# Decoder of twelve sublayers on one core: the last part of the middle sublayers (rank-gated layer, factored attention) stepped between the heads of the second cross attention

## The chip, the cores and the metric

The kernel runs on one core of one Trainium2 chip, in one launch. The metric is the device time in microseconds (us) from launch to end. The core has a matrix engine (TensorE, PE in the profile, with its weight loads as PEld), a vector engine (VectorE, DVE), a scalar engine (ScalarE, ACT), a general engine (GpSimd, POOL) and a queue engine that issues transfers (SyncE, SP). Each engine works through its own list of instructions in the order in which the built program has them. Matrix products land in PSUM, in banks; everything else lives in SBUF.

## The reference

A pre-norm decoder over `x` of shape (8, 256, 128), with a context of shape (8, 512, 128). Every sublayer is `x = x + f(layernorm(x))`:

```
x = x + L0_attn (linear attention)        x = x + L0_xattn (16 heads, context, mask)
x = x + L0_ffn  (8 experts, top 2)
x = x + L1_attn (causal over the 8 batches, rotary)
x = x + L1_xattn (one head, context)
x = x + L1_ffn:  xr, xk = mixes of x and the token before it
                 out = sigmoid(xr Wr) * (relu(xk Wk)^2 Wv)
x = x + L2_attn: qkv = x Wqkv + b; each token sees at most 9 tokens (offsets 0, 1, 2, 4 .. 128)
                 softmax over those, 16 heads of 8, then a projection
x = x + L2_xattn (16 heads of 8, context of 512 keys, no mask)
x = x + L2_ffn  (quantised)
x = x + L3_attn, L3_xattn (16 causal heads each), L3_ffn (3 low-rank blocks)
```

L1_ffn is the rank-gated layer of the title and L2_attn the factored attention. Neither mixes batches: L1_ffn looks one token back in its own batch, L2_attn at most 128 tokens back in its own batch. So batch b of L2_xattn needs only batch b of all that comes before it.

## The kernel before, in words

The running `x` stays in SBUF, and `xt(b)` holds its normalised transpose for batch b. A sublayer ends for a batch with `_norm` (statistics on DVE, the root on POOL, the scaling on DVE) and `_normed` (transposes on PE into `ln_ps`, a copy to `xt` on ACT). The tiles of a sublayer have a two-letter prefix: `moe_` L0_ffn, `ra_` L1_attn, `xa_` L1_xattn, `rk_` L1_ffn, `fa_` L2_attn, `mh_` the head attentions, `qf_` L2_ffn. L0_ffn to L2_attn are called the middle sublayers. Each works in four groups of two batches, and `_middle` runs them as a diagonal: at step s sublayer k does group s - k, the later sublayers first. So L2_attn's four groups come at s = 4 to 7, and at s = 7 only its last group is left. Written as calls, from the end of L0_ffn on: fa(0), rk(1), xa(2), ra(3); fa(1), rk(2), xa(3); fa(2), rk(3); then `E.draining()`, which opens L2_xattn; then fa(3).

A group of L2_attn has four units of 128 tokens. A unit's `weigh` makes q (`fa_qps`, `fa_q`), then up to 9 shifted keys and values, two offsets to a bank (`fa_kvps`): DVE multiplies keys by q (`fa_pr`), ACT copies values (`fa_v`). Then come DVE reductions and a softmax (`fa_sc`, `fa_red`, with an exponential on ACT), and POOL multiplies the values by the weights (`fa_v`). `apply` sums them on DVE (`fa_o`), turns the result (`fa_tps`, `fa_ot`), projects it (`fa_yps`) and adds it to `x`. In the middle the PSUM banks are: three for L0_ffn and then for L2_attn, four for the other sublayers, one for the norms.

L2_xattn is `_heads_attention`. Its loop runs over t = 16 b + h, one head of one batch to a step, 128 steps and 12 more to drain. At step t it computes head t's scores on PE (`mh_sps`) and takes their maxima on DVE (`mh_nm`, two per step); 8 steps later it computes the scores again with the maxima in them (`mh_bsps`) and takes the exponentials on ACT (`mh_e`); 4 steps later, once in four steps, it multiplies by the values (`mh_ops`). Keys, queries and values of batch b+1 are made while batch b runs (`steps`: `mh_kps`, `mh_qps`, `mh_vps`, and transfers on SP that spread them over heads). All of this program's matmuls go through `hd.mm`, which keeps them in program order, and all its other banks come from one pool of two, `hd_g`:

```
self.g = ctx.enter_context(E.tc.tile_pool(name="hd_g", bufs=2, space=PSUM, side="right"))
```

Before its first head, `begin` fills the tiles for keys, queries and values with constants on ACT (`fills`, eight copies from `plain`, four before the first batch's keys and four after), and makes batch 0's keys, values and queries.

The loop can take a guest: a generator of which it runs a few steps between two heads. L0_xattn has one, the rest of L0_attn:

```
normed_already = set(range(B)) if guest is None else {0}
...
        if guest:
            visit(2.4 if t < 9 else 1.4)
```

`visit(r)` adds r to a credit and takes one step of the guest for every whole one. The guest yields a batch's number when that batch's `xt` is ready; before the loop makes batch b+1's queries it runs the guest until that number has come. Order within an engine is otherwise set by the framework's scheduler, from the program order and the dependences.

Of the kernel before, what the change touches and what calls it, by code (L numbers as in the profile page):

```python
# [40 lines left out]
P = 128  # L41
# [176 lines left out]
def _layer_norm(E, b, psum):  # L218
    _normed(E, b, _norm(E, b), psum)


# [235 lines left out]

def _heads_attention(E, ctx, causal=False, mask=None, key_bias=None, gate=False, guest=None):

# [193 lines left out]

    normed_already = set(range(B)) if guest is None else {0}
    credit = [0.0]
# [11 lines left out]
    while t < end or todo:  # L667
        now[0] = t
        b, h = divmod(t, H)
        if b + 1 < B:  # L670
            if h == 0:
                early, spread, values = hd.steps(b + 1)
            if causal:

                at = {2: early[:1], 3: early[1:2], 4: early[2:], 13: [values]}
                at.update({5 + i: spread[i : i + 1] for i in range(6)})
            else:
                at = {6: early[:1], 8: spread[:1], 9: spread[1:2] + early[1:], 13: spread[5:] + [values]}
                at.update({10 + i: spread[2 + i : 3 + i] for i in range(3)})
            if not causal and h == 9:  # L680
                while b + 1 not in normed_already:
                    visit(1)
            for f in at.get(h, ()):
                f()
        if gate and b < B and h == 6:
            gate_of(b)
        if t < H * B:
            maxima(t)
            if t % 4 == 3:
                turn(t // 4)  # L690
        if guest:
            visit(2.4 if t < 9 else 1.4)
        if t % 4 == 1 and 4 < t < H * B + 2:
            turned(t // 4 - 1)
        if 0 <= t - lag < H * B:
            exps(t - lag)
        c = t - lag - 4
        if c % 4 == 0 and 0 <= c < H * B:
            combine(c // 4)
        for f in todo.pop(t, ()):  # L700
            f()
        if t == H * (B - 2) + 12 + free:
            E.draining()
        t += 1
# [50 lines left out]
def _l2_xattn(E, ctx):  # L755
    _heads_attention(E, ctx)

# [255 lines left out]

def _l1_ffn(E, ctx, pg):
    nc, W = E.nc, E.w("L1_ffn")
    one = ctx.enter_context(E.tc.tile_pool(name="rk1", bufs=1, side="right"))
    wk = ctx.enter_context(E.tc.tile_pool(name="rk", bufs=2, side="right"))
    rest = one.tile([P, 2], F32, name="rk_rest")
    for i, n in enumerate(("mu_r", "mu_k")):
        nc.vector.tensor_scalar(rest[:, i : i + 1], W(n), -1.0, 1.0, ALU.mult, ALU.add)  # L1020
    mixed = {}

    def mix(g):
        for i, n in enumerate(("mu_r", "mu_k")):
# [3 lines left out]
            nc.vector.scalar_tensor_tensor(m, E.xt2(g), W(n), t, ALU.mult, ALU.add)  # L1028
            mixed[g, i] = m.rearrange("p b t -> p (b t)")

    def channels(g):
        mr, mk = mixed.pop((g, 0)), mixed.pop((g, 1))
        ps = pg.tile([P, 512], F32, tag="g", name="rk_kps")
        nc.tensor.matmul(ps, W("wk"), mk, start=True, stop=True)
        k = wk.tile([P, 512], F32, name="rk_k")
        nc.scalar.activation(k, ps, AF.Relu)
        nc.scalar.activation(k, k, AF.Square)
        ps = pg.tile([P, 4, D], F32, tag="g", name="rk_rps")
        for t in range(4):
            nc.tensor.matmul(ps[:, t, :], mr[:, t * P : t * P + P], W("wr"), start=True, stop=True)  # L1040
        r = wk.tile([P, 4, D], F32, name="rk_r")
        nc.scalar.activation(r, ps, AF.Sigmoid)
        ps = pg.tile([P, 4, D], F32, tag="g", name="rk_ops")
        for t in range(4):
            nc.tensor.matmul(ps[:, t, :], k[:, t * P : t * P + P], W("wv"), start=True, stop=True)
        nc.vector.tensor_tensor(r, ps, r, ALU.mult)
        for b in range(2):
            E.add(2 * g + b, r[:, 2 * b : 2 * b + 2, :])
            _layer_norm(E, 2 * g + b, E.mid_ln)

    def unit(g):
        mix(g)
        channels(g)

    return unit


def _l2_attn(E, ctx, pg):

# [8 lines left out]
    def weigh(t):  # L1068
# [5 lines left out]
        no = len(offs)  # L1074
        ps = pg.tile([P, D], F32, tag="g", name="fa_qps")
        nc.tensor.matmul(ps, E.xt(b)[:, at], W("wqkv")[:, :D], start=True, stop=True)
        q = wk.tile([P, D], F32, name="fa_q")
        nc.vector.tensor_tensor(q, ps, W("b")[:, :D], ALU.add)

        qb = wk.tile([P, D], F32, tag="fa_s", name="fa_qb")  # L1080
        nc.gpsimd.tensor_tensor(qb, q, W("b")[:, D : 2 * D], ALU.mult)
        pr = wk.tile([P, NO, D], F32, name="fa_pr")
        v = wk.tile([P, NO, D], F32, name="fa_v")
        for i in range(0, no, 2):
            n = min(2, no - i)
            ps = pg.tile([P, 2, 2 * D], F32, tag="g", name="fa_kvps")
            for j in range(n):
                nc.tensor.matmul(ps[:, j, :], E.xt(b, offs[i + j])[:, at], W("wqkv")[:, D:], start=True, stop=True)  # L1088
            nc.vector.tensor_tensor(
                pr[:, i : i + n, :], ps[:, :n, :D], q.unsqueeze(1).to_broadcast([P, n, D]), ALU.mult  # L1090
            )
            nc.scalar.copy(v[:, i : i + n, :], ps[:, :n, D:])  # L1092
        sb = wk.tile([P, H], F32, name="fa_sb")
        nc.vector.tensor_reduce(sb, heads(qb), AX.X, ALU.add)
# [18 lines left out]
    def apply(t):  # L1113
# [3 lines left out]
        nc.vector.tensor_tensor(o, o, W("b")[:, 2 * D :], ALU.add)  # L1117
        ps = pg.tile([P, P], F32, tag="g", name="fa_tps")
        nc.tensor.transpose(ps, o, E.ident)
        ot = wk.tile([P, P], F32, name="fa_ot")  # L1120
        nc.scalar.copy(ot, ps)
        ps = pg.tile([P, D], F32, tag="g", name="fa_yps")
        nc.tensor.matmul(ps, ot, W("wo"), start=True, stop=True)
        nc.vector.tensor_tensor(E.x[:, t, :], ps, E.x[:, t, :], ALU.add)
        if t % 2:
            _layer_norm(E, t // 2, E.mid_ln)

    return lambda g: _pipeline(4, lambda i: weigh(4 * g + i), lambda i: apply(4 * g + i))


def _middle(E, names):


    with ExitStack() as last, ExitStack() as scope, ExitStack() as early:
        banks = lambda to, name, bufs, side="left": to.enter_context(
            E.tc.tile_pool(name=name, bufs=bufs, space=PSUM, side=side)
        )
        E.mid_ln = banks(last, "mid_ln", 1)
        mid = banks(scope, "mid_pg", 4, "right")
        moe = banks(early, "moe_pg", 3) if "L0_ffn" in names else None  # L1140
        units = {}
        for n in names:
            if n != "L2_attn":
                units[n] = MIDDLE[n](E, scope, moe if n == "L0_ffn" else mid)
        for s in range(len(names) + 3):
            for k in reversed(range(len(names))):
                if not 0 <= s - k < 4:
                    continue
                if names[k] == "L2_attn":
                    if s == k:  # L1150
                        early.close()
                        units["L2_attn"] = _l2_attn(E, last, banks(last, "fa_pg", 3))
                    if s == k + 3:
                        scope.close()
                        E.draining()
                units[names[k]](s - k)

# [123 lines left out]
def _l3_ffn(E, ctx):  # L1281
# [90 lines left out]
}  # L1372
MIDDLE = {
    "L0_ffn": _l0_ffn, "L1_attn": _l1_attn, "L1_xattn": _l1_xattn, "L1_ffn": _l1_ffn, "L2_attn": _l2_attn,
}


@with_exitstack
def kernel(ctx: ExitStack, tc: tile.TileContext, ins, at, out, layers=ALL):
# [128 lines left out]

    def prefetch(layer):

        if not small:
            small.append(ctx.enter_context(tc.tile_pool(name="small", bufs=2)))
        if layer in ("L0_ffn", "L3_ffn"):
            load(layer, big.enter_context(tc.tile_pool(name="big", bufs=1)))
        elif layer:
            load(layer, small[0], tag="w")

    if kind(layers[0]) != "L0":
        prefetch(layers[0])
    for i, part in enumerate(parts):  # L1520
        layer, following = part[0], parts[i + 1][0] if i + 1 < len(parts) else None
        E.draining = lambda: begin(following)
        if kind(layer) == "L0":

            def given_up():
                first_w.close()
                prefetch(following)

# [4 lines left out]
        if kind(layer) == "middle":  # L1533
            hd.close()
            E.heads = None
            with tc.tile_pool(name="mid_w", bufs=1) as pool:
                for n in part[1:]:
                    load(n, pool)
                prefetch(following)
                _middle(E, part)  # L1540
            big.close()
            continue
        prefetch(following)
        begin(layer)
# [28 lines left out]
```

## Time and profile before

| | |
|---|---|
| median of 3 runs | 1841.8 us (1839.02 to 1846.99) |
| the profiled execution | 1841.85 us, of which the span from first to last instruction is 1840.1 us |
| busy: PE, DVE, ACT, POOL | 1492.4, 1175.7, 876.6, 489.3 us |
| mean granted TensorE clock | 0.902 |
| first `mh_sps` of L2_xattn | at 1043.8 us |

Times in the trace are us from the start of the span. Rows give the busy time of an engine in a stretch, the mean of one instruction in ns, and the idle time of an engine before a group of instructions with what ended it. Ends of matmuls are modelled, so the distance between two starts is the better measure of what one costs.

### The profile page before, as it was taken

The page shows a single profiled execution, that of the slowest core. Times are in us where ns is not written, and L with a number is a line of the kernel's source. Part 1 is how long each engine was busy: PE and PEld are TensorE (multiplying, and loading weights), DVE is VectorE, ACT ScalarE, POOL GpSimd, SP SyncE. Part 2 cuts the span into 40 slices and gives each one's busy share as a digit, 9 for nine tenths or more (in the row PEclk, how much of TensorE's full clock was granted, in tenths as well). Part 3 has the DMA queues.
Part 4 walks back from the last instruction along what each step waited for, and adds up shares of the span by engine and source line. Part 5 has one row for each costly group of instructions (what it writes and reads, how often), then busy time and mean ns, then how long its engine had stood idle before and what let it go on. Part 6 is the DMA issues. An engine that isn't in the chain of part 4 may idle for free. (4 is left out here: it accounts for less than half of the span.)

```text
span 1840.1 us, 29268 instructions
## 1 busy us (share of the span) xinstructions
PE 1492.4 (81%) x10099; PEld 1071.3 (58%) x10137; DVE 1175.7 (64%) x3843; ACT 876.6 (48%) x1789; POOL 489.3 (27%) x986
## 2 busy tenths in 40 slices
PE   5689999999989988884664689999634999899976
PEld 3466677776655655552453366666413777677753
DVE  4567666666557576788785766666584665455546
ACT  7245445555633434331336266766321666466621
POOL 3222212212101022124233221221225333344321
PEclk9899999999999999886786799999865999899977
DMA  4011101114000000000001021211001321111000
GB/s 149 12 35 34 25 14 36 35 35 156 5 1 1 1 1 1 1 1 0 1 1 34 11 61 37 68 39 37 17 24 54 88 56 48 46 51 49 26 1 23
DMA packets 47235, 60.42 MB, mean 33 GB/s; under 512 B 5232, under 2 KB 36976, under 8 KB 46448
## 3 DMA queue, kind: packets, MB, share of 16 engines
q1 hardware_dynamic: 44720, 56.99, 11.6%
q8 instruction: 80, 1.31, 0.3%
q10 hardware_dynamic: 2368, 1.57, 0.3%
q14 instruction: 67, 0.55, 0.1%
HBM read 14.50 MB, written 1.05 MB: 8 GB/s over the span
## 5 line engine op out<-in xcount | busy, mean ns | idle before, releaser
L443 PE MATMUL mh_sps<-mh_k,mh_q 96*128 96x512 f32 (+2 forms) x1024 | 323.0, 398 | 36.0 <-DMA mh_q<-mh_qp 17.5
L443 PE MATMUL mh_bsps<-mh_q,mh_k 128*128 128x256 f32 (+1 forms) x1536 | 341.3, 327 | 2.8 <-DMA mh_q<-mh_m 1.5
L575 ACT ACTIVATE mh_e<-mh_bsps 128x512 f32<-128x512 f32 x512 | 276.2, 598 | 96.1 <-PE mh_bsps L443 86.5
L443 PEld LDWEIGHTS mh_bsps<-mh_q,mh_k 128*128 128x128 f32 x1536 | 263.6, 194 | 29.7 <-issue 6.5
L443 PEld LDWEIGHTS mh_sps<-mh_k,mh_q 96*128 96x128 f32 x1024 | 172.4, 201 | 89.1 <-issue 34.6
L502 DVE CUSTOM_DVE_ANT_0 mh_rest<-mh_sps,mask_b 128x512 bf16<-128x512 f32 x256 | 167.2, 684 | 82.1 <-PE mh_sps L443 78.9
L443 PE MATMUL mh_ops<-mh_e,mh_v 128*32 128x256 f32 (+1 forms) x3072 | 204.8, 377 | 10.7 <-ACT mh_e L562 10.6
L521 DVE TENSOR_REDUCE mh_nm<-mh_sps 128x1 f32<-128x512 f32 x256 | 159.9, 682 | 59.7 <-PE mh_sps L443 59.7
L443 PEld LDWEIGHTS mh_ops<-mh_e,mh_v 128*32 128x32 f32 x3072 | 97.5, 112 | 82.8 <-ACT mh_e L562 22.0
L562 ACT ACTIVATE mh_e<-mh_bsps 128x384 f32<-128x384 f32 x256 | 116.5, 494 | 49.5 <-PE mh_bsps L443 29.8
L197 POOL TENSOR_SCALAR ln_rstd<-ln_mv 128x2 f32<-128x2 f32 x96 | 22.5, 237 | 412.7 <-DVE ln_mv L195 402.0
L502 DVE CUSTOM_DVE_ANT_0 mh_rest<-mh_sps,km_q 128x128 bf16<-128x128 f32 (+1 forms) x256 | 80.0, 350 | 66.3 <-PE mh_sps L443 64.5
L502 DVE CUSTOM_DVE_ANT_0 mh_rest<-mh_sps,causal 128x128 bf16<-128x128 f32 (+1 forms) x256 | 79.5, 353 | 63.1 <-PE mh_sps L443 46.0
L528 POOL CAST mh_hi<-mh_nm 128x8 fp32r<-128x8 f32 x128 | 24.6, 192 | 333.6 <-DVE mh_nm L502 203.8
L215 ACT COPY xt<-ln_ps 128x256 f32<-128x256 f32 x96 | 36.2, 377 | 151.1 <-PE ln_ps L214 99.0
L214 PE MATMUL ln_ps<-ident,ln_z 128*128 128x128 f32 x100 | 30.3, 370 | 84.4 <-DVE ln_z L201 82.1
L605 ACT COPY mh_osb<-mh_ops 128x256 f32<-128x256 f32 x128 | 47.7, 373 | 102.4 <-PE mh_ops L443 102.3
L1088 PE MATMUL fa_kvps<-w_L_attn,xt 128*128 128x256 f32 x272 | 83.6, 457 | 13.6 <-ACT fa_v L1092 10.3
L540 ACT CAST mh_m<-mh_mps 8x256 fp32r<-8x256 f32 x128 | 46.3, 362 | 98.4 <-PE mh_mps L446 95.8
L443 PE MATMUL mh_bsps<-mask_t,ident 128*128 128x512 bf16 x219 | 85.2, 389 | 0.4 <-ACT mh_e L575 0.4
L863 ACT ACTIVATE moe_si<-moe_gps 128x512 f32<-128x512 f32 x64 | 38.0, 597 | 97.8 <-PE moe_gps L861 74.1
L214 PEld LDWEIGHTS ln_ps<-ident,ln_z 128*128 128x128 f32 x100 | 15.2, 162 | 107.1 <-DVE ln_z L201 62.3
(339 smaller groups left out, 3166.3 us busy)
## 6 DMA issues: line engine op xcount, KB each, us to landing
mh_k<-mh_kp SPq DMA_DIRECT2D x64, 256.0 KB
mh_q<-mh_qp SPq DMA_DIRECT2D x256, 64.0 KB
mh_k<-mh_kp SPq DMA_DIRECT2D x64, 128.0 KB
w_L_ffn<-in_w_L_ffn SPq DMA_DIRECT2D x2, 1558.0 KB
w_L_attn<-in_w_L_attn SPq DMA_DIRECT2D x2, 1056.0 KB
ctx_t<-in_ctx_t SPq DMA_DIRECT2D x4, 512.0 KB
mh_q<-mh_m ACTq DMA_DIRECT2D x128, 8.0 KB
w_L_ffn<-in_w_L_ffn SPq DMA_DIRECT2D x2, 687.0 KB
```

What stands on the lines that cost most here:

```text
L214: E.nc.tensor.transpose(ps[:, q, :], z[:, q, :], E.ident)
L215: E.nc.scalar.copy(E.xt(b), ps.rearrange("p q t -> p (q t)"))
L443: return self.E.tc.keep_in_program_order(self.E.nc.tensor.matmul(*a, **kw))
L502: nc.vector.tensor_tensor_reduce(rest[:, : scores.shape[1]], scores, lowered, -1.0, -FLOOR, ALU.add, ALU.min, accum_out=at)
L521: nc.vector.tensor_reduce(u.nm[:, c, col], ps, AX.X, ALU.max, negate=True)
L528: nc.gpsimd.tensor_copy(hi, nm)
L540: nc.scalar.copy(m, ps[:8].rearrange("p c q -> p (c q)"))
L562: nc.scalar.activation(e, ps, AF.Exp, scale=scale)
L575: nc.scalar.activation(e, ps, AF.Exp, scale=scale)
L605: nc.scalar.copy(osbs[b][:, u4 % 2, :], ops)
L863: nc.scalar.activation(si, pgate, AF.Silu)
L1088: nc.tensor.matmul(ps[:, j, :], E.xt(b, offs[i + j])[:, at], W("wqkv")[:, D:], start=True, stop=True)
```

## The change

`_l1_ffn` and `_l2_attn` become generators that yield between pieces: L2_attn after the queries, after each bank of keys and values and around the projection; L1_ffn after the mix, after each product and around the norms. `_middle` writes its order out: the diagonal as it was up to fa(0), then rk(1), xa(2), ra(3), xa(3). The rest, fa(1), rk(2), fa(2), rk(3), fa(3), is left in one generator, `E.guest`, and L2_xattn runs it between its heads, with batches 0 and 1 known as ready. In that part the tiles come from `hd_g` and the matmuls go through `hd.mm`. L1_ffn's work tiles have one buffer in place of two. L2_xattn is opened when `_middle` has returned, no longer before fa(3). The weights of all middle sublayers are loaded in L0's last part, ahead of L0_ffn's own, where they came after them.

```diff
-def _heads_attention(E, ctx, causal=False, mask=None, key_bias=None, gate=False, guest=None):
+def _heads_attention(E, ctx, causal=False, mask=None, key_bias=None, gate=False, guest=None, known=(0,)):
...
-    normed_already = set(range(B)) if guest is None else {0}
+    normed_already = set(range(B) if guest is None else known)
...
-            visit(2.4 if t < 9 else 1.4)
+            visit(2.4 if t < 9 and 1 not in known else 1.4)
...
 def _l2_xattn(E, ctx):
-    _heads_attention(E, ctx)
+    guest, E.guest = E.guest, None
+    _heads_attention(E, ctx, guest=guest, known=(0, 1))
...
-def _l1_ffn(E, ctx, pg):
+def _l1_ffn(E, ctx, side="left"):
-    wk = ctx.enter_context(E.tc.tile_pool(name="rk", bufs=2, side="right"))
+    wk = ctx.enter_context(E.tc.tile_pool(name="rk", bufs=1, side=side))
...
+        yield
+        mr, mk = mixed
+        ps = E.banks.rk.tile([P, 512], F32, tag="g", name="rk_kps")
+        E.mm(ps, W("wk"), mk, start=True, stop=True)
...
         for b in range(2):
             E.add(2 * g + b, r[:, 2 * b : 2 * b + 2, :])
-            _layer_norm(E, 2 * g + b, E.mid_ln)
+            zs.append(_norm(E, 2 * g + b))
+        yield
+        yield
+        for b in range(2):
+            _normed(E, 2 * g + b, zs[b], E.banks.ln, E.turn_over)
+            yield
...
-            ps = pg.tile([P, 2, 2 * D], F32, tag="g", name="fa_kvps")
+            ps = E.banks.fa.tile([P, 2, 2 * D], F32, tag="g", name="fa_kvps")
...
             nc.scalar.copy(v[:, i : i + n, :], ps[:, :n, D:])
+            yield
...
-            _layer_norm(E, t // 2, E.mid_ln)
+            z = _norm(E, t // 2)
+            yield
+            yield
+            _normed(E, t // 2, z, E.banks.ln, E.turn_over)
+            yield t // 2
...
+    _run(fa(0))
+    _run(rk(1))
+    xa(2)
+    ra(3)
+    xa(3)
...
+    def rest():
+        g = E.heads.g
+        E.mm, E.turn_over = E.heads.mm, E.heads.turn_over
+        E.banks = SimpleNamespace(fa=g, rk=g, ln=g)
+        rk = _l1_ffn(E, last)
+        for steps in (fa(1), rk(2), fa(2), rk(3), fa(3)):
+            yield from steps
+        last.close()
+        E.close_weights()
```

## The prediction

> **What bounds the kernel now.** I read the page first, then the busy time by stretches, the waits of DVE, and the timeline where L2_xattn opens. On the page the slices are 46 us each:
>
> ```profile
> PE   5689999999989988884664689999634999899976
> ...
> DVE  4567666666557576788785766666584665455546
> ...
> PEclk9899999999999999886786799999865999899977
> ```
>
> PE is full in slices 3 to 10 (L0) and 23 to 27 (L2_xattn), and thin between 17 and 22, where DVE carries the most and the PE clock sags. The thin part is where the moved work stands. By stretches (columns: length; busy time and instructions of each engine; granted clock; DMA):
>
> ```profile
> core 0: us, PE busy (x) PEld busy (x) DVE busy (x) ACT busy (x) POOL busy (x), PEclk, DMA share, GB/s
> 831.00:1043.80 212.80, 114.94 (x432) 81.27 (x432) 153.21 (x379) 74.42 (x139) 72.17 (x88) 0.74 0.03 8
> 1043.80:1194.00 150.20, 140.92 (x1104) 97.27 (x1108) 104.56 (x201) 95.39 (x194) 32.78 (x89) 0.95 0.22 53
> 1194.00:1318.00 124.00, 114.73 (x968) 79.08 (x960) 76.64 (x169) 78.73 (x164) 25.85 (x70) 0.96 0.12 30
> ```
>
> Up to 831 us all engines have the same work in the same order in both programs. From there to L2_xattn's first `mh_sps` at 1043.8, DVE leads (153 of 213) and still waits a good deal. In L2_xattn PE leads (141 of 150) and a third of DVE is free. What DVE waits for in the first stretch (total, times, longest):
>
> ```profile
> DVE fa_pr L1089 <- PE fa_kvps L1088: 17.5, 15, 9.6
> DVE ln_z L201 <- POOL ln_rstd L198: 14.3, 13, 3.4
> DVE fa_o L1115 <- POOL fa_v L1110: 11.1, 8, 2.8
> DVE x L1124 <- PE fa_yps L1123: 5.7, 7, 1.8
> ```
>
> The chain of the factored attention goes round all four engines, and DVE stands at each turn. The last view is the opening of L2_xattn (start, length; fills and first keys on ACT, spreads on SP, first scores on PE):
>
> ```profile
> 969.74 3.60 ACT L363 CAST mh_k<-plain 64x4096 fp32r<-64x4096 f32 x1 [0.74 <-DVE ln_mv L195]
> 983.40 0.69 ACT L409 ACTIVATE mh_kf<-mh_kps,w_L_xattn 128x512 f32<-128x512 f32 x1
> 989.75 5.31 SPq L422 DMA_DIRECT2D mh_q<-mh_qp  x8
> 1043.83 7.16 PE L443 MATMUL mh_sps<-mh_k,mh_q 96*128 96x512 f32 x12 [0.46 <-ACT xt L215]
> ```
>
> It is ready near 997 and then waits for fa(3). In the changed program nothing covers this opening.
>
> **1. When L2_xattn starts.** What is left before it: ra(3), xa(3), the opening. ra(3) ended at 878.1 (the last `ln_z` of its batch 7). After 861.5 about 4.4 us of DVE rows ahead of that point are fa(1)'s (a 1.21 and some twelve of 0.2 to 0.4 us); they go, and two `xa_nm` of 0.6 come ahead. So about 875. xa(3)'s second batch then has no cover: norm and copy 0.8; queries 0.5 + 0.5; scores 0.7; maximum 0.7 + 0.15; two exponentials of 0.69 + 0.19; transposes, copies and products 0.6 + 0.59 x 2 + 0.9; hops 2. That is 10 to 11: the last `xa_et` near 886. Then the fills before the keys, three of 3.60 and one of 0.75: 897.5. From the first `mh_kf` to the queries' spread the trace has 989.75 - 983.40 = 6.35; from that spread to the first scores 6.6 (L0_xattn: 57.44 to 64.04, where PE waits for it). First `mh_sps` near 911 instead of 1043.8: **133 us earlier**. The second set of fills (11.5 us of ACT) ends by then. I give this +-10.
>
> **2. What moves into L2_xattn.** fa(1) to fa(3) are 12 units, rk(2) and rk(3) two groups, with 10 norms.
> - DVE: of the 153 in the first stretch ra(3) keeps 28.7, xa(3) 6.8, the quantised layer's preparations 3, and 9 of 19 norms 12. The rest, 103, moves; call it 105. Rows: `fa_o` 23.9, `fa_pr` 21.3, the `fa_sc` reduction 15.3, short ones 38, rk 11, norms 13, less what overlaps.
> - PE: start to start a `fa_kvps` takes 0.2155 at full clock (10 in 2.32 us from 956.92), so 204 take 44; 112 of 128 columns at 0.11 take 12, `rk_kps` 1.7: 58.
> - ACT: 54 `fa_v` copies 18.5, exponentials and turns 7, norms 4, rk 2.5, table loads for two sigmoids 5: 37 onto 95.
> - POOL: 12 `fa_v` of 2.16 = 25.9, `fa_qb` 5, roots 9: 40 onto 33.
> - SP: the guest issues no transfer. The middle weights pass ahead of L0_ffn's in SP's queue near 430 us; L0_ffn begins near 515, so this costs nothing.
>
> The guest has 32 yields per group of L2_attn and 7 per group of L1_ffn: 3 x 32 + 14 = 110, at 1.4 a step 78.6 steps. In the built order the last `fa_yps` stands before step 78, and batches 2 to 7 come before they are asked for. So the guest lies in the first 79 of 140 steps, which today last 1043.8 to about 1194: 150 us. The remaining 124 stay.
>
> **3. How long those 79 steps become.** Floors: PE 137 (141 less the slow clock of the first 12 us) + 58 = 195. DVE 105 + 105 = 210. ACT 132, POOL 73. So **DVE takes the bound from PE**, narrowly. To the floor come DVE's waits, as its order has the next link right behind: after each exponential the reduction, after POOL's product `fa_o`, after the projection `x`. From the rows above: `fa_pr` 7.9 (without the 9.6 behind the fills), `ln_z` 7.5 (10 of 19 norms), `fa_o` 11.1, `x` 5.7, the rest 3: 35. What waits behind DVE are the `mh_nm`, and behind these PE, which has three banks for scores. A few `mh_nm` now stand between the links and cover part; but the exponential now queues behind `mh_e` of 0.60 on ACT. Bounds: 0 if all is covered, 70 if each wait doubles. I take 30: 210 + 30 = 240, **90 longer**.
>
> [...] `rk_t` takes 0.39 to 0.48 alone, 2.25 and 1.71 where it runs beside POOL's `fa_v` of 2 us (at 942.4 and 887.0). [...] By the row, collisions cost some 4 us in the first stretch, already in the durations. [...]
>
> [...] By start distances PE's steady batch has 29.3 of 31.0 us filled, so I count all 58. [...]
>
> **Sum.** 1841.85 - 133 + 90 = **1799 us**. The profiled execution (1841.85) is the median (1841.8) of the runs. 0.5%, about what a measurement tells from no change, is 9 us.
>
> **The rivals.**
> *Packed:* the maxima fill every wait of the chain, as L0_xattn's guest seems to allow (64 to 415 us: PE 320 of 351, its waits on the guest some 15). Then the floor of 210 holds: +60, time 1769. Against: there DVE has 236 of 351; here 210 of 210. Chance 0.12.
> *Two banks decide (slower):* in `hd_g` the guest takes a bank 106 times (90 in the units, 6 for rk, 10 norms), the heads 59 times in 79 steps: 165. Two banks then allow 2 x 240 / 165 = 2.9 us for each. Break-even is 150 + 133 = 283 us, a mean hold of 3.4. A `fa_kvps` bank is held from 931.49 to 933.39, 1.9 us with DVE and ACT free; behind a few `mh_nm` (0.68) and `mh_e` (0.60) it may be 4. If the mean gets to 3.7 the 79 steps last 305: +155, time 1864. PE stands still then, since `mh_sps` is behind `fa_kvps` in its order. Against: only 54 of 165 takings are `fa_kvps`; transposes, queries and maxima hold 1 to 2 us; and L0_xattn fitted 208 takings into 351 us (3.4 each) with PE full. Chance 0.14 for this or DVE waits as large.
> *A late opening:* if the fills wait longer for the space of the middle's tiles and the first scores come only at 930, 1818; within the range.
> *The move does not happen:* excluded, the built order has `fa_` and `rk_` between `mh_sps`.
>
> **Chances.** Main case 0.68 (1775 to 1825), packed 0.12, slower 0.14, and 0.06 between 1825 and 1851. Over 0.5% faster (below 1832.6): 0.68 + 0.12 and little of the last, less 0.02 of the main case's tail: 0.78. Within: 0.08. Slower: 0.14. The range 1766 to 1838 takes in the packed case and the ends of the opening and of DVE's waits, and leaves out the slower case and a sliver below.
>
> **What would show it.** First `mh_sps` at 901 to 921; from there 225 to 260 us to the last `fa_yps`; DVE busy at least 0.85 of these with `mh_nm` waiting for PE far less than today's 59.7 us in the stage; PE's granted clock at 0.95 or more there; POOL beside DVE without long `mh_nm`. Wrong if: `fa_kvps` on PE waits for `fa_v` or `fa_pr` by tens of us (banks), DVE is below 0.75 busy, or the first `mh_sps` comes after 930.

## The result, and the profile after

The changed kernel takes 1849.8 us (median of 11 runs, 1847.5 to 1852.6) against 1840.0 us for the kernel before (11 runs, 1835.7 to 1847.0): a ratio of 1.0049, 95% interval 1.0037 to 1.0061. Forecast was 1799, in a range of 1766 to 1838. The move took place and the first scores of L2_xattn came 123 us earlier; all of that was given back in the steps that hold the moved work.

The page of the changed kernel, 40 slices of 46 us:

```profile
PE   5689999999989988882476878789734999899976
...
DVE  4567666666557576787296867776584665455546
...
PEclk9899999999989999885788989799865999799977
```

Where the page of before had a thin part and then a full one, there is now a short hole (PE 2 and 4, 832 to 924 us) and then seven slices in which neither row is full: PE at 6 to 8, DVE at 6 to 9. That is the thing to notice, since the forecast had DVE at the bound there. By stretches (columns as before: length; busy time and instructions of PE, PEld, DVE, ACT, POOL; granted clock; DMA):

```profile
core 0: us, PE busy (x) PEld busy (x) DVE busy (x) ACT busy (x) POOL busy (x), PEclk, DMA share, GB/s
831.00:920.90 89.90, 30.91 (x119) 17.98 (x117) 43.74 (x99) 35.30 (x38) 30.00 (x35) 0.67 0.07 17
920.90:1206.80 285.90, 222.53 (x1459) 164.75 (x1460) 212.81 (x468) 131.89 (x295) 77.44 (x142) 0.88 0.13 29
1206.80:1323.00 116.20, 107.78 (x921) 75.12 (x919) 74.95 (x169) 82.17 (x167) 24.04 (x66) 0.97 0.12 29
```

The second line is the guest's stretch, from L2_xattn's first scores to the last projection of fa(3). In the kernel before, the same 79 steps of the heads took 150.2 us (1043.8 to 1194.0). By spans: first scores 122.9 earlier, the 79 steps 135.7 longer (285.9 - 150.2), everything after them 4.9 shorter (1848.0 - 1206.8 against 1840.1 - 1194.0): +7.9, which is 1848.0 - 1840.1.

What PE waits for in that part (total, times, longest; window 910 to 1260):

```profile
PE fa_tps L451 <- DVE fa_o L1127: 29.4, 4, 8.6
PE ln_ps L451 <- DVE ln_z L201: 17.8, 10, 3.2
PE mh_sps L448 <- DMA mh_q<-mh_qp: 11.9, 2, 10.3
...
PE mh_sps L448 <- DVE mh_nm L527: 4.6, 4, 2.5
PE mh_mps L451 <- ACT fa_v L1101: 4.5, 4, 2.3
PE fa_kvps L448 <- DVE x L1135: 2.0, 2, 1.4
PE fa_kvps L448 <- ACT fa_v L1101: 1.1, 2, 0.8
```

47 us stand at two links, both transposes of something that the guest's chain has just made: `fa_tps` turns `fa_o`, `ln_ps` turns `ln_z`. (The 10.3 of `mh_sps` is the opening.) In the last three lines PE waits for one of the two shared banks, until ACT or DVE has read it out; with the smaller lines of this kind, not shown, that comes to some 11 us, read by what ended each wait. Now the same view for DVE:

```profile
DVE mh_nm L527 <- PE mh_sps L448: 62.7, 37, 20.4
DVE fa_o L1125 <- POOL fa_v L1120: 9.7, 6, 2.7
DVE x L1514 <- PE mh_yps L448: 9.0, 4, 5.2
DVE ln_z L201 <- POOL ln_rstd L198: 7.4, 9, 2.0
DVE mh_rs L628 <- PE mh_otps L451: 5.9, 7, 1.2
DVE fa_pr L1098 <- PE fa_kvps L448: 4.7, 12, 0.7
DVE fa_red L1116 <- ACT fa_sc L1115: 3.2, 8, 0.5
DVE fa_sb L1104 <- POOL fa_qb L1090: 1.6, 3, 0.5
```

The chain's own waits on DVE (9.7, 7.4, 4.7, 3.2, 1.6) come to 27, near the 30 that the forecast put there. The big one is `mh_nm` on `mh_sps` (20.4 of it is the opening): DVE waits for the heads' scores, and these stand behind a transpose in PE's order. The two engines wait for each other in turn. One place, row by row (start, length; in brackets the idle time before and what ended it):

```profile
981.13 0.49 PE L448 MATMUL fa_yps<-w_L_attn,fa_ot 128*128 128x128 f32 x2 [0.69 <-ACT fa_ot L1131]
981.37 1.34 DVE L1107 TENSOR_REDUCE fa_sc<-fa_pr 128x144 f32<-128x1152 f32 x1
...
984.35 0.39 DVE L1116 TENSOR_REDUCE fa_red<-fa_sc 128x16 f32<-128x144 f32 x1 [0.39 <-ACT fa_sc L1115]
...
985.51 2.18 POOL L1120 TENSOR_TENSOR fa_v<-fa_v,fa_sc 128x1152 f32<-128x1152 f32 x1 [4.80 <-DVE fa_sc L1118]
987.73 2.08 DVE L1125 TENSOR_REDUCE fa_o<-fa_v 128x128 f32<-128x1152 f32 x1 [2.36 <-POOL fa_v L1120]
989.85 0.29 DVE L1127 TENSOR_TENSOR fa_o<-fa_o,w_L_attn 128x128 f32<-128x128 f32 x1
990.20 0.47 PE L451 MATMUL fa_tps<-ident,fa_o 128*128 128x128 f32 x1 [8.58 <-DVE fa_o L1127]
```

This is the last unit of fa(1). Between its last keys and its `fa_tps` the code yields only once more, in the `apply` of the unit before it, so in PE's order this `fa_tps` stands right behind the `fa_yps` of that unit. From 981.4 to 990.2 one engine works at a time, DVE, ACT, DVE, POOL, DVE, and PE does nothing for 8.58 us, although the heads' next products wait for nothing of their own: `mh_bsps` starts 0.13 us after it, at 990.33. Three of the four waits at `fa_tps` are such last units (8.58, 7.52, 8.41). The units before the last mostly do not do this (the fourth wait, 4.87, is one), because the next unit's queries and keys, with their yields and the heads between, stand between a unit's softmax and its `apply`.

### The profile page after: what moved, and what is told of

It is laid out like the page before. It is cut to its first block, busy times and chain, and to the rows that moved or that the text cites. A ratio compares the mean times of both kernels' runs of the same rounds, so it can differ in the third digit from the quotient of the medians.

```text
span 1848.0 us, 29287 instructions
## 1 busy us (share of the span) xinstructions
PE 1484.2 (80%) x10137; PEld 1073.4 (58%) x10137; DVE 1174.6 (64%) x3845; ACT 877.4 (47%) x1791; POOL 490.1 (27%) x986
## 5 line engine op out<-in xcount | busy, mean ns | idle before, releaser
L448 PE MATMUL mh_bsps<-mh_q,mh_k 128*128 128x256 f32 (+1 forms) x1536 | 354.4, 337 | 4.0 <-DMA mh_q<-mh_m 2.6
L581 ACT ACTIVATE mh_e<-mh_bsps 128x512 f32<-128x512 f32 x512 | 280.0, 599 | 109.7 <-PE mh_bsps L448 101.4
L448 PEld LDWEIGHTS mh_bsps<-mh_q,mh_k 128*128 128x128 f32 x1536 | 270.2, 201 | 29.4 <-issue 6.7
L527 DVE TENSOR_REDUCE mh_nm<-mh_sps 128x1 f32<-128x512 f32 x256 | 164.3, 683 | 71.4 <-PE mh_sps L448 71.1
L448 PE MATMUL mh_bsps<-mask_t,ident 128*128 128x512 bf16 x256 | 99.6, 389 | 0.4 <-ACT mh_e L581 0.4
L214 PE MATMUL ln_ps<-ident,ln_z 128*128 128x128 f32 x68 | 20.6, 369 | 73.6 <-DVE ln_z L201 73.5
L201 DVE TENSOR_SCALAR ln_z<-x,ln_mv,ln_rstd 128x128 f32<-128x128 f32 x128 | 45.9, 401 | 49.5 <-POOL ln_rstd L198 49.3
L867 PE MATMUL moe_ups<-xt,w_L_ffn 128*128 128x512 f32 x128 | 69.9, 628 | 6.9 <-ACT moe_si L869 4.8
```

The source lines that it names most:

```text
L201: (engine or nc.vector).tensor_scalar(z[:, q, :], E.x[:, 2 * b + q, :], mv[:, q, 0:1], rstd[:, q : q + 1], ALU.subtract, ALU.mult)
L448: return self.E.tc.keep_in_program_order(self.E.nc.tensor.matmul(*a, **kw))
L527: nc.vector.tensor_reduce(u.nm[:, c, col], ps, AX.X, ALU.max, negate=True)
L581: nc.scalar.activation(e, ps, AF.Exp, scale=scale)
L867: nc.tensor.matmul(ps, W("w13")[:, o : o + P], xt, start=True, stop=True)
```

## The experiments

Each changes a few lines of L2_xattn or of its guest. *A* is the theory that the loss is PE standing in its program order at these links, with too many links to a head besides. Its rivals: DVE's sum of work is the bound; the two banks; the bare opening.

For the comparison, the stage in each kernel from its first to its last `mh_sps` (column "stage"; idle is the stage less PE's busy time; time is the median, with one run where no interval stands). The columns from "stage" on are of the one profiled execution. It took 1836.0 in e7 and 1829.7 in e4, 6 and 8 us from the median; in the others it is within 3. A single run can be off by some us as well: the 20 runs of e4 spread over 14.

| kernel | time | ratio to before | stage | PE busy | idle | clock |
|---|---|---|---|---|---|---|
| before | 1840.0 | | 253.4 | 238.5 | 14.9 | 0.95 |
| changed | 1849.8 | 1.0037 to 1.0061 | 386.8 | 316.6 | 70.2 | 0.90 |
| e1: links apart, same steps | 1839.6 | 0.9984 to 1.0011 | 374.8 | 322.3 | 52.5 | 0.91 |
| e2: lower rate | 1834.8 | 0.9961 to 0.9982 | 369.2 | 308.5 | 60.7 | 0.91 |
| e3: light maxima | 1825.6 | one run | 363.4 | 304.2 | 59.2 | 0.92 |
| e5: links apart, rate 1.4 | 1805.8 | 0.9792 to 0.9831 | 341.8 | 304.6 | 37.2 | 0.96 |
| e7: last unit apart only | 1829.7 | 0.9927 to 0.9978 | 366.6 | 314.6 | 52.0 | 0.91 |
| e8: more banks | 1857.5 | one run | 390.0 | 318.5 | 71.5 | 0.91 |
| e9: constant transposes | 1832.7 | one run | 360.8 | 311.2 | 49.6 | 0.93 |
| e12: e9 at a lower rate | 1819.6 | 0.9868 to 0.9907 | 349.3 | 306.0 | 43.3 | 0.95 |
| e10: other steps between | 1807.8 | 0.9787 to 0.9834 | 344.2 | 305.1 | 39.1 | 0.95 |
| e11: e5, light maxima | 1798.2 | one run | 337.3 | 300.6 | 36.7 | 0.95 |
| e4: fa(1) at the opening | 1837.4 | 0.9966 to 0.9991 | 339.7 | 291.4 | 48.3 | 0.91 |
| e6: e4, links apart, rate 1.0 | 1821.0 | 0.9876 to 0.9925 | 326.1 | 288.1 | 38.0 | 0.94 |

(In e4 and e6 the stage begins at 949 and 950 instead of some 921, and holds 8 units instead of 12.)

**e1, e2, e5: apart, thinner, and both.** The links are set apart with empty yields, in which the heads go on:

```diff
         for i in range(5):
             if i < 4:
                 yield from weigh(4 * g + i)
+            if i == 4:
+                for _ in range(5):
+                    yield
             if i:
                 yield from apply(4 * g + i - 1)
...
             z = _norm(E, t // 2)
-            yield
-            yield
+            for _ in range(4):
+                yield
```

(and likewise for the norms of L1_ffn). That makes 141 yields in place of 110. e1 raises the rate to 1.78 a step, so that the guest still lies in 79 steps; e5 keeps 1.4, so that it spreads over 101; e2 has the changed kernel's guest at 1.12 a step, 98 steps.

> Empty steps put between the links of the guest's chain: five before the last unit's apply of each group of L2_attn, two more at every norm; the rate is raised from 1.4 to 1.78 so that the guest still ends near step 79. No work is added or removed. Theory A (PE stands, in its own order, at fa_tps and ln_ps until DVE and POOL have gone through the chain, with the heads' scores behind it): the waits of PE at fa_tps (29.4 us between 910 and 1260) and ln_ps (17.8) fall below 10 each, the clock of the stretch rises from 0.88, the first 79 steps shrink from 286 to 225-245 us, the time is 1795 to 1812. Theory B (the two banks of hd_g): nothing is gained, 1845 to 1855. Theory C (DVE's load of some 210 us with its own waits): at most 10 us gained.

> The changed kernel with the guest's rate lowered from 1.4 to 1.12 steps per head, nothing else: the same links at the same distance in steps of the guest, over some 99 heads' steps in place of 79. Theory A: the norms' waits at ln_ps fall by about half (2 guest steps are then 1.8 heads' steps), the waits at fa_tps of each group's last unit stay (there is no guest step between its last keys and its fa_tps), so 5 to 15 us are gained. Theory B and theory C (too much per step for two banks, or for DVE): both are thinned by a fifth, 20 to 40 us are gained.

> The empty steps of e1_spaced_same_steps with the rate left at 1.4, so the guest ends near step 101. Theory A: the waits fall as there and the load is spread too; the stretch to step 101 gains 50 to 70 us against the changed kernel, the time is 1785 to 1805. Theory B: 1815 to 1830, from the spreading alone.

e1 gains 10 us on the changed kernel, far less than *A* expected and what the rival of DVE's load allowed. Its PE waits in the guest's stretch (921 to 1188.5):

```profile
PE mh_sps L448 <- DVE mh_nm L527: 11.5, 8, 3.5
...
PE fa_tps L451 <- DVE fa_o L1127: 7.3, 2, 3.7
PE fa_yps L448 <- ACT fa_ot L1131: 5.8, 7, 3.1
```

`fa_tps` went from 29.4 to 7.3 and the norms' wait to a few us, but others came in their place, for the maxima and for `fa_ot`. e2 gains 15, with its waits at `fa_tps` nearly as before (27.4 in all): there are fewer links to a head, and each last unit still costs 6.5 to 9.1 us. e5 gains 44, the slow end of what *A* expected but more than the two together, and is 1.9% faster than the kernel before:

```profile
923.20:1202.50 279.30, 247.33 (x1778) 181.00 (x1779) 235.84 (x522) 157.91 (x351) 88.22 (x168) 0.96 0.15 36
...
PE fa_tps L451 <- DVE fa_o L1127: 6.3, 2, 4.7
PE mh_sps L448 <- DVE mh_nm L527: 4.2, 8, 1.1
```

The same 279 us hold the whole guest and 101 steps of the heads, where the changed kernel needs 286 for 79. Over the stage the 45 us (386.8 - 341.8) split into 33 of idle PE (70.2 - 37.2) and 12 of PE's busy time for the same 2240 matmuls (316.6 - 304.6), with the clock at 0.96 against 0.90. How much of the 12 the clock made is not shown: at 0.91, e2 has 308.5 busy and e1 322.3. The distance alone, in the same steps, took 18 us from PE's idle time, and PE's busy time grew by 6; with room between the links the idle time fell by 33.

**e7: one half of the distance.** The 5 yields before a group's last `apply`, without those of the norms; rate 1.4.

> One half of e5_spaced_rate_1_4: the 5 empty yields before a group's last apply, while the norms keep their 2 yields; rate 1.4 unchanged. Theory A: fa_tps's wait (29 us) goes, ln_ps's (18 us) stays, and the guest is thinned by 15 yields (125 instead of 110): half to two thirds of e5's gain of 44, so 1820 to 1830. If spacing is what counts and thinning not, near 1815; if thinning is what counts (e5 thins by 28 %, this by 14 %), near 1828.

1829.7, 20 of the 44, at the slow end of what *A* expected and also near the 1828 that thinning alone was to give, so e7 does not part the two. `fa_tps` waits 13.5 over the stage and `ln_ps` 12.0, in five waits of 0.8 to 4.9 us. The other 24 come with the norms' 2 more yields each: in e5 these waits at `ln_ps` are 2.1 and those at `fa_tps` 6.3, and the guest is thinner (89 steps here, 101 in e5).

**e9: no wait at the two links.** The transposes turn the identity; everything else is computed as before. The middle's fa(0), rk(0) and rk(1) share the code, and the first scores come 5 us later (926.2).

```diff
-        E.turn_over(ps, o)
+        E.turn_over(ps, E.ident)
...
-            _normed(E, t // 2, z, E.banks.ln, E.turn_over)
+            _normed(E, t // 2, E.ident.unsqueeze(1).to_broadcast([P, 2, D]), E.banks.ln, E.turn_over)
```

> The changed kernel, but fa_tps turns the identity instead of fa_o, and the norms of L1_ffn and L2_attn turn the identity instead of ln_z. Everything is still computed and nothing is left out, but TensorE no longer waits for VectorE at these two links (its order stays). Theory A (TensorE stands in its program order at these two links and loses clock while it stands): the 47 us of waits go and the granted clock of the guest's stretch rises from 0.88 to 0.93 or more, which takes another 10 us of TensorE's busy time; the guest's stretch falls from 286 to about 235 and the time to 1795 to 1805. Rival (VectorE carries the stretch; TensorE's waits only show it): as the same VectorE work stays, the waits move to mh_sps and fa_kvps, and the time stays at 1835 or more.

Between the two, and nearer to the rival's 1835 than to *A*'s 1805: 1832.7, a gain of 17. From the first scores to the last projection, and PE's waits in that stretch:

```profile
926.20:1183.00 256.80, 214.53 (x1458) 158.71 (x1459) 207.81 (x464) 130.44 (x295) 75.78 (x140) 0.93 0.13 32
...
PE mh_sps L448 <- DVE mh_nm L527: 21.2, 12, 5.2
```

The stretch falls from 285.9 to 256.8, so 29 us of it are the two links, with PE's busy time 8 us shorter at the higher clock (0.93 against 0.88). Some 17 of their 47 us come up again at the next scores, behind the maxima (21.2 against 4.6). *A*'s size was too high; the rival's "stays" is wrong too.

**e12: both at once.** e9 with e2's rate.

```diff
-            visit(2.4 if t < 9 and 1 not in known else 1.4)
+            visit(1.12 if 1 in known else 2.4 if t < 9 else 1.4)
```

> Both at once: the transposes of a constant (as e9_transposes_of_a_constant) and the changed kernel's guest at 1.12 yields a step instead of 1.4 (as e2_lower_rate, 98 steps). No empty yields: the links stand as near as in the changed kernel, but TensorE does not wait at them. Alone the two gave 17 and 15. Theory A (distance of the links and a thinner guest are two separate terms, and the empty yields of e5 bring nothing else): near e5, 1800 to 1815. If e5's gain lies in something else that its empty yields do (DVE's and ACT's order, the banks), the two add up to no more than 1818 to 1830.

1819.6: the two gains of 17 and 15 add up (30) and do not reach e5, as the rival had it (1818 to 1830). So distance does something that cutting the link does not. The trace of e12 shows what is left, in the guest's stretch 18.0 us of PE waiting for `mh_nm` where e5 has 4.2:

```profile
PE mh_sps L448 <- DVE mh_nm L527: 18.0, 15, 2.4
```

One such place:

```profile
995.01 2.20 POOL L1120 TENSOR_TENSOR fa_v<-fa_v,fa_sc 128x1152 f32<-128x1152 f32 x1 [0.69 <-DVE fa_sc L1118]
...
997.24 2.12 DVE L1125 TENSOR_REDUCE fa_o<-fa_v 128x128 f32<-128x1152 f32 x1 [0.64 <-POOL fa_v L1120]
...
999.28 0.68 DVE L527 TENSOR_REDUCE mh_nm<-mh_sps 128x1 f32<-128x512 f32 x1
...
1000.01 0.50 PE L448 MATMUL mh_sps<-mh_k,mh_q 96*128 96x512 f32 x1 [2.29 <-DVE mh_nm L527]
```

DVE stands in program order as well. It waits for POOL with the maximum behind it, then reduces `fa_o` for 2.1 us, and the scores' banks are not read meanwhile. Five of the stage's eight waits over 1 us for a maximum in e12 end within 3.3 us of such a reduction's start. That this is the 14 us between e12 and e5 fits the two rows of waits (18.0 and 4.2); it was not tried by itself.

**e10: real work in place of empty yields.** rk(2)'s steps stand before the last `apply` of fa(1), rk(3)'s before that of fa(2); 131 yields at 1.3 a step, 101 steps.

```diff
...
-        for steps in (fa(1), rk(2), fa(2), rk(3), fa(3)):
+        for steps in (fa(1, rk(2)), fa(2, rk(3)), fa(3, [None] * 5)):
             yield from steps
```

> As e5_spaced_rate_1_4, but the last apply of a group of L2_attn is held off by real work and not by empty yields: the steps of rk(2) stand before the last apply of fa(1), those of rk(3) before that of fa(2); before that of fa(3) stay 5 empty yields, and norms keep 4. That is 131 yields, at 1.3 a step 101 steps, as thin as e5. Theory A: the distance between the links counts, not what stands in it: within 8 us of e5 (1806), so 1798 to 1814; fa_tps's wait below 10 us. If it was the empty steps as such (pauses in which the heads catch up), the fa_tps wait of fa(1) and fa(2) comes back and the time is 1820 or more.

1807.8, 2 us from e5. `fa_tps` waits 4.7 in all. Distance counts, and it need not be empty.

**e3 and e11: is DVE's sum the bound?** The maxima are taken over 128 of 512 columns; the other scores are left out of them.

```diff
-                nc.vector.tensor_reduce(u.nm[:, c, col], ps, AX.X, ALU.max, negate=True)
+                nc.vector.tensor_reduce(u.nm[:, c, col], ps[:, :128], AX.X, ALU.max, negate=True)
```

> The changed kernel with the maxima of L2_xattn's scores taken over the first 128 of 512 columns: that leaves out three quarters of these reductions' work, some 0.4 us of 0.68 for each, 65 us of DVE in the first 79 steps. Theory C (DVE binds): the 79 steps fall from 286 to about 225 us. Theory A: the chain's own rows are as long as before and PE still stands at fa_tps and ln_ps; 5 to 25 us are gained, from maxima that stood ahead of links. Theory B: under 15 us.

> e5_spaced_rate_1_4 with the maxima taken over the first 128 of 512 columns (VectorE's rows fall from 0.68 to about 0.3 us; the rest of the scores is left out of the maximum). Asks what bounds the stage once the links are apart. TensorE as the bound (busy 305 of 342 there): little to win, 1795 to 1803. VectorE as the bound (281 of 342): its load falls by some 100 us over the stage, and the stage by 20 or more: 1785 or less.

The stage in the changed kernel, in e3 and in e11 (columns as above):

```profile
921.10:1307.90 386.80, 316.58 (x2240) 231.55 (x2240) 285.80 (x628) 203.28 (x439) 99.62 (x203) 0.90 0.13 30
919.00:1282.40 363.40, 304.19 (x2238) 225.37 (x2238) 190.61 (x628) 200.50 (x438) 99.30 (x203) 0.92 0.14 32
919.90:1257.20 337.30, 300.57 (x2238) 223.99 (x2238) 190.50 (x628) 200.81 (x438) 99.53 (x203) 0.95 0.15 35
```

On the changed kernel (e3) DVE's busy time falls by 95 us (285.8 to 190.6) and the stage by 23; `fa_tps` still waits 21.7. On e5 (e11) it falls by 91 (from 281.4), and the stage by 4.5. A bound by DVE's sum would have given most of that back; e3's own 23 us show that the length of the maxima is a part of the loss while the links stand close. In e11 the stage is 337 with 300.6 of PE busy and DVE at 190.5: once the links are apart, PE is what the stage is full of.

**e8: banks.** The turned maxima and the guest's norms get a PSUM bank of their own, taken from the second scores.

```diff
-    ps_b = ctx.enter_context(E.tc.tile_pool(name="mh_pb", bufs=3, space=PSUM))
+    ps_b = ctx.enter_context(E.tc.tile_pool(name="mh_pb", bufs=2 if 1 in known else 3, space=PSUM))
+    pm = ctx.enter_context(E.tc.tile_pool(name="mh_pm", bufs=1, space=PSUM)) if 1 in known else pg
...
```

> Tests the rival of the two banks on the changed kernel: the heads' turned maxima and the guest's norms get a PSUM bank of their own (taken from the three of the second scores, which have two in L2_xattn), so of the 165 takings of the two shared banks in the guest's steps some 29 leave, and a bank is free sooner. Theory A: PE stands at fa_tps and ln_ps for their data and not for a bank: the stretch of the guest keeps 280 to 290 us and the time 1845 to 1860 (the two banks of the second scores may cost some). Bank rival: with 18 % fewer takings the stretch falls by 18 % of what lies above the floor and more, 30 us or so: 1820.

1857.5 with a guest's stretch of 287.1 (285.9 without), and the waits at `fa_tps` are no shorter:

```profile
PE fa_tps L451 <- DVE fa_o L1129: 31.3, 5, 8.8
```

Relieving the two shared banks changed nothing for the better. (The taken bank may have cost some: `mh_bsps` waits 4.6 for `mh_e`.)

**e4 and e6: the opening.** fa(1) runs before the heads while L2_xattn opens, as it did in the kernel before; e6 adds the distances and takes 1.0 yields a step.

```diff
...
+    if then in HEADS:
+        E.draining()
+        _run(fa(1))
     psum.close()
...
-        for steps in (fa(1), rk(2), fa(2), rk(3), fa(3)):
+        for steps in (rk(2), fa(2), rk(3), fa(3)):
             yield from steps
```

> fa(1) runs before the heads, while L2_xattn opens, as it does in the kernel before; only rk(2), fa(2), rk(3), fa(3) are left to the steps between the heads, at 1.4 a step as in the changed kernel (78 yields, 56 steps). The rest is the changed kernel. Theory A (links of the chain too near each other in PE's order, and too many of them per head): the links stand as near as before, so each unit costs what it costs in the changed kernel: the guest's 56 steps take about 2/3 of the overhead, and the opening's empty PE is used by fa(1) at its old price of some 30 us. Total 1825 to 1845: a gain of 5 to 20 on the changed kernel. Theory C (what the prediction missed is the opening: nothing covers it, and its slow clock and the late first scores cost the time): 1800 or less.

> As e4_fa1_at_opening, with the empty yields of e5_spaced_rate_1_4 (5 before a group's last apply, norms 4 instead of 2) and 1.0 yields a step: the guest of 100 yields lies over 100 steps with 8 units instead of 12. Theory A: as thin as e5 but a third lighter, so PE's waits for the chain nearly vanish, and the heads' PE of 252 us plus 40 is the floor of the stage; first scores some 30 us later than in e5. Total 1790 to 1810, about e5's 1806 or a little better. If what e5 has left over is due to the bare opening, it should beat e5 by 10 or more; if it is due to PE's own work, the two are the same within 5.

e4 is 12 us faster than the changed kernel, with a third of its guest gone and `ln_ps` still at 16.0. e6 is 15 us slower than e5, against what was expected: the first scores come 27 us later (950.0 for 923.4) and the stage is only 16 shorter (326.1 for 341.8). With the links apart, fa(1) was cheaper between the heads than at the opening (the two runs differ in the rate too). The bare opening is not where the time went.

## Why the prediction was wrong

**Step 1, the start, came out at the edge of its margin.** 911 +- 10 was forecast, 921.1 came. The opening of the changed kernel:

```profile
897.07 3.60 ACT L368 CAST mh_k<-plain 64x4096 fp32r<-64x4096 f32 x1 [1.71 <-DVE x L1014]
...
908.87 0.68 ACT L414 ACTIVATE mh_kf<-mh_kps,w_L_xattn 128x512 f32<-128x512 f32 x1
...
921.14 1.19 PE L448 MATMUL mh_sps<-mh_k,mh_q 96*128 96x512 f32 x2 [10.31 <-DMA mh_q<-mh_qp]
```

From the first `mh_kf` to the scores it took 12.3 (forecast 12.95). The ten us were lost ahead of it. ra(3)'s last `ln_z` ended at 878.6 and not near 875; then four `xa_et` follow each other, at 886.8, 889.1, 891.4 and 894.8, where the working had two and the last near 886; and the fills began at 897.1.

**Step 2, the moved work, was right for DVE, ACT and POOL.** For the guest's stretch DVE has 212.8 (forecast floor 210), ACT 131.9 (132), POOL 77.4 (73). PE has 222.5 at a clock of 0.88, where the forecast had 195 at about the full clock. 195 / 0.88 is 222, but that the clock makes the whole difference is the author's estimate; no run shows it.

**Step 3 failed: "I take 30: 210 + 30 = 240".** It is 285.9, so 136 longer where 90 was forecast. The floor stood (212.8), and the waits on top of it were 73 and not 30. The chain's own waits on DVE, for which the 30 was meant, were 26 in this stretch. The rest is a term that the step put at nothing: DVE waiting for the heads' products, some 32 for scores (`mh_nm`, without the opening) and 12 for the heads' outputs. The step took the chain's waits from the rows of DVE, because DVE "stands at each turn", and asked whether the maxima would fill them. It said that PE stands behind DVE and did not follow PE's own order through the guest. There a link waits with all the heads' work behind it, and no maximum can fill DVE's time while PE makes no scores. e9 puts 29 of the 46 us at these links. The remaining 17 fit the waits left in e9 (21.2 for maxima), which would be DVE's own order of chain and maxima; no run removes these alone, so that part stays open. The size could be had from rows of one unit: 1.34 + 0.30 + 0.38 + 0.31 + 0.32 + 0.39 + 0.25 + 0.31 on DVE and ACT, 2.18 on POOL, 2.08 + 0.29 on DVE: 8.2 us with nothing else going on, three times, is 25 of the 29.4 at `fa_tps`.

**The clock was counted at full speed ("0.95 or more").** It was 0.88. The expectation failed with the waits: the clock is lowest, 0.74, in the two stretches of 20 us that hold waits of 8.58 and 7.52 (last section).

**DVE beside POOL's products**, for which the forecast added nothing, has one row that is much longer, at one of the twelve products in the guest's stretch, and on another instruction than the `rk_t` of the forecast. `ln_z`, of which half of all on DVE take at most 0.35 us, takes 1.98 there:

```profile
1171.14 1.96 POOL L1120 TENSOR_TENSOR fa_v<-fa_v,fa_sc 128x1024 f32<-128x1024 f32 x1
1171.20 1.98 DVE L201 TENSOR_SCALAR ln_z<-x,ln_mv,ln_rstd 128x128 f32<-128x128 f32 x1 [0.35 <-POOL ln_rstd L198]
1173.23 0.73 PE L451 MATMUL ln_ps<-ident,ln_z 128*128 128x128 f32 x2 [3.07 <-DVE ln_z L201]
```

That is 1.6 us, and it stands in a wait of PE. Beside the other products DVE has maxima (two in 1.28 to 1.29), other short instructions at their usual length (`x` 0.28, `fa_pr` 0.42), or nothing. `rk_t` takes 0.49 both times (before, up to 2.25), but no product runs beside it. So adding nothing was right; why this one `ln_z` took so long is not shown.

**PE's 58 us** of moved work were all counted, and that was right: even in e11, with DVE busy only 190.5 of 337.3 us, the stage is 84 us longer than before's 253.4, PE's busy time 62 longer.

**The rivals.** *Packed* did not come: it needed PE to keep feeding DVE. *Two banks* did not decide: some 11 us of waits, and e8. The break-even of 283 us is 273 with the start 10 us later; 285.9 is 13 over it, of which 5 came back after the guest's end. The case of "DVE waits as large" had the nearest size, but as a rider on another mechanism, so that is luck. Of the signs named beforehand, DVE at 0.74 (below 0.75), the clock at 0.88, and `mh_nm` waiting 71.1 us in the stage and not far less than 59.7 said "wrong"; the one for banks stayed silent.

## What to carry to other kernels

When work is threaded between other work on engines that run in program order, walk the order of each engine and ask at every link of the guest's chain what stands behind it; a sum of busy times and the waits of one engine do not show it. Put as many steps between two links as the chain is long (here 8 us, some 3 steps of a head at e5's 2.8 us each), and thin the guest to match: apart or thinner alone brought 10 to 15 us, both brought 44. Why both together bring more than their sum is only in part shown (e12). If other work of the guest is at hand to stand in the gap, as rk(2) was here, it serves as well as an empty step.

## What the runs showed of the hardware

Of the fourteen stretches of 20 us from 921 on in the changed kernel, the granted clock is lowest (0.74, 0.74 and 0.80) in the three that hold the longest waits at `fa_tps` (8.58, 7.52 and 8.41 us). Six of them (columns as above; the clock is the third figure from the end):

```profile
941.00:961.00 20.00, 14.95 (x96) 12.08 (x97) 18.06 (x36) 9.04 (x22) 4.23 (x8) 0.83 0.29 70
...
981.00:1001.00 20.00, 10.39 (x66) 6.42 (x66) 10.72 (x23) 5.47 (x14) 4.67 (x6) 0.74 0.01 2
...
1061.00:1081.00 20.00, 16.74 (x133) 12.56 (x131) 15.43 (x38) 9.32 (x22) 7.28 (x13) 0.91 0.32 73
1081.00:1101.00 20.00, 11.62 (x75) 8.13 (x75) 11.71 (x23) 6.88 (x18) 3.63 (x6) 0.74 0.02 5
...
1161.00:1181.00 20.00, 16.93 (x107) 13.14 (x109) 15.78 (x33) 9.87 (x22) 6.89 (x13) 0.83 0.15 35
1181.00:1201.00 20.00, 11.29 (x88) 8.15 (x84) 14.11 (x26) 8.20 (x22) 3.84 (x6) 0.80 0.21 47
```

The two stretches at 0.74 are those with the waits of 8.58 and 7.52 us at `fa_tps`; that of 8.41 lies in the one at 0.80 and that of 4.87 in the first, at 0.83. The one at 0.91 has waits of at most 3.23, but the stretch from 1161 has 0.83 with a longest wait of 3.07. So these runs do not show from what length on a wait goes with a lower clock. How much time the lower clock took is not shown either: from the changed kernel to e5 PE's busy time for the same matmuls fell by 12 us of the 45, with the clock from 0.90 to 0.96, but e1 and e2 differ by 14 at the same 0.91.
